# Attending in one bank, a rest behind a root, key features by blocks of 432 and an early bias in an attention kernel

## The chip, the cores and the metric

The kernel runs on one core of one Trainium2 chip. A core has a matrix engine (TensorE: PE for the products, PEld for loading the stationary side), a vector engine (VectorE, DVE), an engine for functions (ScalarE, ACT), a general engine (GpSimd, POOL) and an engine that here only issues transfers (SyncE, SP); 16 DMA engines move data between the device memory and the core's own memory. Products are written to PSUM, which is used in banks of 512 fp32 numbers for each of 128 partitions. The metric is device time in microseconds (us) from the first to the last instruction of one launch; lower is better. All arithmetic here is fp32.

## The reference, cut to what matters

Eight images of 128 channels and 36 x 36 pixels pass through two layers. Layer 0 is an attention between convolutions. Layer 1 turns the image into N = 1296 tokens of C = 128 numbers, attends additively over all pairs of tokens and sends the result through experts that pick their tokens:

```python
# layer 1, attention (x is the normalized token t)
q = einsum('bld,ed->ble', x, Wq) + bq
k = einsum('bld,ed->ble', x, Wk) + bk
t = tanh(q[:, :, None, :] + k[:, None, :, :])
scores = einsum('bijd,d->bij', t, w) + bw[0]
attn = softmax(scores, axis=-1)
return einsum('bij,bjd->bid', attn, x)

# layer 1, experts (E = 64, hidden 512, K = 8 tokens for each expert)
probs = softmax(einsum('bsd,ed->bse', x, gate_w) + gate_b, axis=1)
vals, idx = top_k(probs.transpose(0, 2, 1), K)
gathered = x[flat_idx].reshape(Bn, K, E, Dn)
pooled = einsum('bked,bke->bed', gathered, topv)
h = gelu(einsum('ebd,edh->ebh', [pooled, 1], weight1))
out = einsum('ebh,eho->ebo', [h, 1], weight2)
outputs[b, flat_idx] += out * topv
```

The tanh of a sum over 128 channels for each of 1296 x 1296 pairs is most of the work, and with it the scores.

## The kernel before

**How the tanh becomes products.** With exponentials of the key and of the query, tanh(q + k) is a quotient: for each pair and channel a numerator and a denominator, both sums of few products. The channels' features lie in NF = 8 blocks of 128 rows. For a key tile and a block, TensorE forms the denominators `d` and the numerators `n` of several channels at once, as small products with 32 or 64 rows; ACT takes the logarithm of `d` and the exponential of its negative (`lq`, lines 972 and 975), VectorE multiplies `n` by it (`rp`, line 1003), and POOL adds up the products (line 1012), VectorE for a few slots (lines 997 and 999). The sum gives the scores of one key tile, and ACT its exponential `e` (line 1032).

**Tiling.** The queries of an image are cut into 3 chunks of CH = 432, each of 4 query tiles of T = 108. The keys are cut into KT = 11 tiles, ten of 128 and a rest of REM = 16. A unit is a chunk against a key tile; it has 12 slots (the rest 2). The loop runs over all slots, 2,928 in all. In slot p it calls `numerators(p)` and `denominators(p + LAG)` and `terms`, then gives other work a turn.

**PSUM.** The pool `ps_d` holds the denominators, two tiles of two banks. The pool behind `ps_n` has four banks: a slot takes two for its `n`, and all other work takes its banks from the same pool by `aux(...)`. A bank is handed round when its readers are done.

**Other work, woven in.** Generators do everything that is not a slot, and say at each `yield` what they want next: `step(rest)` and `TAKE` ask for a turn without matmuls, `matmuls(rest)` for one with them; `rest` is the number of slots to wait at least. Four lanes (`first_of_all`, `urgent`, `gates`, `background`) hold the generators. In each slot `take_turns` runs every lane that is due without matmuls, before the numerators, and `matmul_turn` at most one portion of matmuls, behind the denominators, against a budget of 400 columns per slot. `bmm` (line 284) and `turned_to` (line 288) issue a product or a transposition and count its columns. An fp32 product is two matmul instructions in the trace.

**The generators that matter here.**

- `tokens(b)` makes the tokens of the next image, stores them (`tokd`) and leaves normalized tokens `xh` (with a column of ones), their transposition `xT` and the rest's rows `xr`.
- `keys(b, tiles)` (line 667): for each key tile and each half of the feature blocks, four products `pk` of 128 rows by the tile's columns, side by side in one bank, an exponential on ACT (line 687) into `ks`, and a store to `kd` in the device memory, laid out by key tile. For the rest tile POOL multiplies `ks` by two constants (line 692) and only the two products are stored. `made` holds the tiles that are done. `prefetch(u)` (line 926) loads the features `kf` of a unit two units ahead.
- `attend(b, c, es)` runs when all 11 `e` of a chunk are there. It loads the chunk's tokens from `tokd` (four loads on SP), and for each of 4 query tiles `weigh` (line 737) sums the 11 products of `e` and `xh` in two parts of 6 and 5 key tiles, each in a bank `pa` of its own: VectorE copies the first part to `sums` (line 770), adds it to the second (line 772), and adds the sum, divided by its column of ones, to the tokens in `t2` (line 775).
- `attend_early` does nine of the eleven key tiles of the very last chunk while the loop still runs, in two parts as well.
- `gate_logits` (line 793) normalizes the chunk again: POOL takes the inverse root of the variances as a power (`rsqrt`, line 265), TensorE turns `t2` twice, VectorE copies it to `t2T` (line 820, which is stored to `t2d`), normalizes it (line 830) and gets the gate's logits. `gate_tokens` (line 850) makes the softmax, the top 8, the weights `gt` of the chosen tokens (all others zero; stored to `gd`) and the pooled tokens. For the last image the subtraction that gives `gt` is on VectorE.

**The tail.** After the loop, `urgent.run` gives one turn to what is left of `urgent`. Then nine of the 32 expert weights of 1 MB are requested on SP (`load_next`, line 1173), the biases, and what is left of `urgent` is drained. `gates` and `res` are read back for the final sum, and `gate_tokens(7)` runs. In the loop over groups of four experts `inner` forms the first product for a group (a bias by the product with `which`, line 1231, then four products) and its gelu, `turned` transposes, `outer` makes the second product; every weight that is used up makes room for the next. At the end the results are spread over the tokens (`pf`), added to `res` and stored image by image.

Of the kernel before, what the change touches and what calls it, by code (L numbers as in the profile page):

```python
# [23 lines left out]
T = 108  # L24
# [46 lines left out]
def kernel(  # L71
# [43 lines left out]

    kd = [dram.tile([NKT, 128, NF * 128], F32, tag=f"kd{b % 2}", name=f"kd{b}") for b in range(NB)]
    tokd = [dram.tile([N, C], F32, tag=f"tokd{b % 2}", name=f"tokd{b}") for b in range(NB)]
# [12 lines left out]
    with ExitStack() as loop, ExitStack() as score:  # L130
# [455 lines left out]

        prepared, made = {}, set()

# [77 lines left out]

        def keys(b, tiles):

            xT = prepared[b][1]
            yield matmuls(1)  # L670
            for t in tiles:
                o, n = KT[t]
                first = (b, t) == (0, order[0])
                if first:
                    kf_of[0] = kfp.tile([128, NF, 128], F32, tag="kf", name="kf")
                for q0 in (0, NF // 2):
                    some = slice(q0, q0 + NF // 2)
                    pk = aux("pk1").rearrange("p (q t) -> p q t", t=128)
                    for q in range(NF // 2):
                        bmm(pk[:, q, :n], a_k[:, (q0 + q) * 128 : (q0 + q + 1) * 128],  # L680
                           xT[:, o : o + n], start=True, stop=True)
                    yield TAKE
                    if first:
                        ks = kf_of[0][:, some, :]
                    else:
                        ks = kstp.tile([128, NF // 2, 128], F32, tag="ks", name="ks")
                    nc.scalar.activation(ks[:, :, :n], pk[:, :, :n], AF.Exp)
                    kd3 = kd[b][t].rearrange("p (q t) -> p q t", t=128)[:, some, :]
                    if n == REM:

                        for x in range(2):
                            nc.gpsimd.tensor_scalar(
                                ks[:, :, (x + 1) * n : (x + 2) * n], ks[:, :, :n],
                                pairs[:, min(q0, 1), x : x + 1], None, ALU.mult,
                            )
                        nc.sync.dma_start(kd3[:, :, : 2 * n], ks[:, :, n : 3 * n])
                    else:
                        nc.sync.dma_start(kd3, ks)
                    if q0 > 0:
                        made.add((b, t))  # L700
                    yield matmuls()

# [17 lines left out]
        def attend_early(b, c, es):  # L720

            xh, _, xr = prepared[b]
            held = [chunk_tile("sums") for _ in range(TPC // 2)]
            for i in range(TPC):
                at = (i % 2) * (C + 1)
                sums = early[i] = held[i // 2][:T, at : at + C + 1]
                for some in (order[:5], order[6 : NKT - 2] + order[5:6]):
                    pa = aux("pa1")[:T, : C + 1]
                    weigh(pa, i, some, es, xh, xr)
                    yield TAKE  # L730
                    if some[0] == order[0]:
                        nc.vector.tensor_copy(sums, pa)
                    else:
                        nc.vector.tensor_add(sums, pa, sums)
                    yield matmuls()

        def weigh(pa, i, some, es, xh, xr):

            for j in some:
                if j < NKT - 1:  # L740
                    e, v = es[j][:, i * T : (i + 1) * T], xh[:, j, :]
                else:
                    rows = slice(32 * i, 32 * i + REM)
                    e, v = es[j][rows, :T], xr[rows]
                bmm(pa, e, v, start=(j == some[0]), stop=(j == some[-1]))

        def attend(b, c, es):


            xh, _, xr = prepared[b]  # L750
            if c == 0:
                t2 = big_tile("t2").rearrange("p (t c) -> p t c", c=128)
                mv = two.tile([T, NT, 2], F32, tag="t2_mv", name="t2_mv")
                attended[b] = (t2, mv)
            t2, mv = attended[b]
            own = range(c * TPC, (c + 1) * TPC)
            for at in own:
                nc.sync.dma_start(t2[:T, at, :], tokd[b][at * T : (at + 1) * T])
            for i, at in enumerate(own):
                if i in early:  # L760
                    parts, sums = (order[NKT - 2 :],), early[i]
                else:
                    parts = (range(6), range(6, NKT))
                    sums = two.tile([T, C + 1], F32, tag="sums", name="sums")
                for some in parts:
                    pa = aux("pa1")[:T, : C + 1]
                    weigh(pa, i, some, es, xh, xr)
                    yield TAKE
                    if some[0] == 0:
                        nc.vector.tensor_copy(sums, pa)  # L770
                        yield matmuls()
                nc.vector.tensor_add(pa, pa, sums)
                inv = small.tile([T, 1], F32, tag="inv", name="inv")
                nc.vector.reciprocal(inv, pa[:, C : C + 1])
                nc.vector.scalar_tensor_tensor(
                    t2[:T, at, :], pa[:, :C], inv, t2[:T, at, :], ALU.mult, ALU.add
                )
                st = small.tile([T, 6], F32, tag="t2_st", name="t2_st")
                nc.vector.bn_stats(st, t2[:T, at, :])
                nc.vector.bn_aggr(mv[:, at, :], st)  # L780
                yield matmuls()
            if c == NCH - 1:
                prepared.pop(b)
            if b == NB - 1:
                yield from gate_logits(b, [c])
# [7 lines left out]
        def gate_logits(b, chunks):  # L793
# [23 lines left out]
            for c in chunks:  # L817
# [3 lines left out]
                nc.sync.dma_start(t2d[b][:, c * CH : (c + 1) * CH], tt)  # L821
                yield matmuls(1)
                for j0 in range(0, TPC, 2):
# [26 lines left out]
        def gate_tokens(b):  # L850
# [24 lines left out]
            yield step(2)  # L875
            (nc.vector if b == NB - 1 else nc.gpsimd).tensor_sub(gt, pr, gt)
            nc.sync.dma_start(gd[b], gt)
            yield matmuls(3)
            half = NT // 2
            gT = []  # L880
# [45 lines left out]
        def prefetch(u):  # L926
            if u < len(units) and u not in kf_of:
                b, c, j = units[u]
                assert (b, j) in made
                n = 128 if j < NKT - 1 else 32  # L930
                kf = kfp.tile([128, NF, 128], F32, tag="kf", name="kf")
                nc.sync.dma_start(
                    kf[:, :, :n], kd[b][j].rearrange("p (q t) -> p q t", t=128)[:, :, :n]
                )
                kf_of[u] = kf
# [164 lines left out]
        a_q, a_k, cs_s, fb_s, eb_s = (feat[n] for n in ("a_q", "a_k", "cs_s", "fb_s", "eb_s"))  # L1100
        drain(tokens(0), keys(0, order[:1]))
        for i, q in enumerate(IN_TURN):
# [4 lines left out]
        for p in range(LAG):  # L1107
            denominators(p)
        drain(keys(0, order[1:3]))
        prefetch(1)  # L1110
        urgent.append(keys(0, order[3:]))
        pending = deque()
        for p, (u, k) in enumerate(slots):
            b, c, j = units[u]
            rem = j == NKT - 1
            if k == 0:
                prefetch(u + 2)
                if c == 0 and j == 1:
# [4 lines left out]
                    if b + 1 < NB:  # L1123
                        background.extend(
                            (normal(b + 1), conv_keys(b + 1), layer0(b + 1), tokens(b + 1),
                             keys(b + 1, range(NKT)))
                        )
# [56 lines left out]
        urgent.run(len(slots))  # L1184
        for _ in range(9):
            load_next()
        b1_s = biases.tile([E, HID], F32, tag="b1", name="b1_s")
        nc.sync.dma_start(b1_s, weight1[:, 128, :])
        b2_s = biases.tile([128, O], F32, tag="b2", name="b2_s")
        for h in range(2):  # L1190
            nc.sync.dma_start(b2_s[E * h : E * (h + 1)], weight2[:, HID, :])
        drain(*urgent)

# [10 lines left out]
        res.append(big_tile("res")[:, :N])  # L1204
        nc.sync.dma_start(res[4], t2d[4])
        drain(gate_tokens(NB - 1))

# [15 lines left out]
    def inner(g):  # L1223
        ph = aux("phid")

        of_group = ident[:E, g * EG : (g + 1) * EG].rearrange("p (q x) -> p q x", x=1)
        which = hidp.tile([E, EG * 32], F32, tag="which", name="which")
        nc.gpsimd.tensor_copy(
            which.rearrange("p (q x) -> p q x", q=EG), of_group.to_broadcast([E, EG, 32])
        )  # L1230
        mm(ph, which, b1_s, start=True, stop=False)
        for q in range(EG):
# [51 lines left out]
    for h in range(NB // 2):  # L1284
        for c in range(NCH):
# [5 lines left out]
            for i in range(2):  # L1291
                r = res[2 * h + i][:, cols]
                nc.vector.tensor_add(r, pfs[i], r)
        for b in (2 * h, 2 * h + 1):
            nc.sync.dma_start(out[b], res[b])

# [61 lines left out]
```

The softmax here doesn't subtract the row's maximum and nothing guards it: scores larger than these inputs give would overflow.

## Time and profile before

| | us |
|---|---|
| median of three runs (lowest, highest) | 6137.45 (6137.38, 6148.23) |
| the profiled execution | 6140.74 |
| its span, from the first to the last instruction | 6139.0 |
| the loop over the slots in it | 162 to 5986 |
| the first and the last request for a weight of the tail | 5987.38 / about 6094 |
| end of the last addition of results on VectorE | 6132.96 |

The mean granted clock of TensorE was 0.985 of full speed. The costliest groups of instructions (busy us, mean ns of one, then idle time before them and what ended most of it):

```
L1012 POOL TENSOR_TENSOR accp<-accp,rp 128x864 f32<-128x864 f32 x1440 | 2915.8, 2025 | 1041.0 <-DVE rp L1003 948.8
L949 PE MATMUL n<-qf,kf 32*128 32x432 f32 (+1 forms) x11520 | 3325.3, 574 | 46.5 <-ACT e L1032 13.3
L949 PE MATMUL d<-qf,kf 32*128 32x432 f32 (+1 forms) x11520 | 2991.6, 561 | 38.7 <-ACT lq L972 38.2
L972 ACT ACTIVATE lq<-d 128x864 f32<-128x864 f32 x2928 | 2524.2, 878 | 542.6 <-PE d L949 512.1
L1003 DVE TENSOR_TENSOR rp<-n,lq 128x432 f32<-128x432 f32 x3912 | 2173.3, 600 | 743.5 <-PE d L949 542.8
```

A line starts with the line of code, the engine and the operation, then what is written and read, the shape and the number of instructions. Matmuls overlap each other, so their busy time and their means are larger than what one adds to the time. Idle time of an engine that doesn't set the pace costs nothing.

### The profile page before, as it was taken

The numbers are of one execution on the slowest core, as the hardware profiler recorded it, in microseconds if no ns is written. First come the engines' busy times: TensorE is split into PE (matmuls) and PEld (weight loads), VectorE is DVE, ScalarE is ACT, GpSimd is POOL, SyncE is SP. The second block draws the span as 40 slices with busy tenths as digits, with TensorE's granted clock in tenths as the row PEclk, the third lists the DMA queues.
The fourth block names the chain that finished last, engine by engine and source line by source line (L and its number), as shares of the span: only waits on it lengthen the run. The fifth ranks groups of instructions, "written<-read, shape, count | busy, mean of one in ns | idle before, by whom it ended". The sixth has DMA issues, their size and how long they took to land.

```text
span 6139.0 us, 93072 instructions
## 1 busy us (share of the span) xinstructions
PE 5957.9 (97%) x33480; PEld 2862.1 (47%) x33480; DVE 4796.4 (78%) x9521; ACT 5279.9 (86%) x5371; POOL 4597.7 (75%) x2819
## 2 busy tenths in 40 slices
PE   7999999999999999999999999999999999999996
PEld 5454444544544445444455444454444544544443
DVE  4787878877788787877888777887778877788882
ACT  1888898888988888889998889888898888999990
POOL 4777777777787777778778786877777777787870
PEclk9999999999999999999999999999999999999997
DMA  1210011100110002100111001110011100110008
GB/s 44 70 37 22 25 62 38 34 25 28 68 43 20 26 27 71 39 24 23 44 55 39 22 24 59 44 39 22 20 65 40 34 25 28 58 50 29 28 20 297
DMA packets 151519, 270.87 MB, mean 44 GB/s; under 512 B 45648, under 2 KB 76752, under 8 KB 151056
## 3 DMA queue, kind: packets, MB, share of 16 engines
q1 hardware_dynamic: 151056, 264.92, 13.0%
q8 instruction: 264, 4.33, 0.3%
q14 instruction: 199, 1.63, 0.1%
HBM read 200.41 MB, written 64.19 MB: 43 GB/s over the span
## 4 chain that ended last, share of the span: by engine, by line
PE 77%; ACT 7%; DVE 6%; issue 6%; POOL 2%; DMA 1%; SPq 0%; DVEq 0%; POOLq 0%; ACTq 0%
PE n L949 37%; PE d L949 12%; PE pa L284 7%; PE pc L284 5%; ACT lq L972 5%; PE s L284 3%; PE pk L284 3%; PE pq L284 3%; DVE rp L1003 2%; DVE n L997 1%; DVE accd L999 1%; PE d L954 1%; ACT lq L975 1%; DMA w<-in_weight_dram 1%; PE n L954 1%
## 5 line engine op out<-in xcount | busy, mean ns | idle before, releaser
L1012 POOL TENSOR_TENSOR accp<-accp,rp 128x864 f32<-128x864 f32 x1440 | 2915.8, 2025 | 1041.0 <-DVE rp L1003 948.8
L949 PE MATMUL n<-qf,kf 32*128 32x432 f32 (+1 forms) x11520 | 3325.3, 574 | 46.5 <-ACT e L1032 13.3
L949 PE MATMUL d<-qf,kf 32*128 32x432 f32 (+1 forms) x11520 | 2991.6, 561 | 38.7 <-ACT lq L972 38.2
L972 ACT ACTIVATE lq<-d 128x864 f32<-128x864 f32 x2928 | 2524.2, 878 | 542.6 <-PE d L949 512.1
L1003 DVE TENSOR_TENSOR rp<-n,lq 128x432 f32<-128x432 f32 x3912 | 2173.3, 600 | 743.5 <-PE d L949 542.8
L975 ACT ACTIVATE lq<-lq 128x1728 f32<-128x1728 f32 (+1 forms) x1464 | 2398.2, 1638 | 46.3
L949 PEld LDWEIGHTS n<-qf,kf 32*128 32x128 f32 (+1 forms) x11520 | 1206.4, 184 | 1600.3 <-DVE rp L1003 581.5
L949 PEld LDWEIGHTS d<-qf,kf 32*128 32x128 f32 (+1 forms) x11520 | 1090.0, 185 | 422.1 <-issue 224.7
L997 DVE TENSOR_TENSOR n<-n,lq 128x432 f32<-128x432 f32 x1440 | 814.9, 608 | 142.1 <-PE n L949 88.5
L999 DVE TENSOR_TENSOR accd<-n,accd 128x432 f32<-128x432 f32 x1440 | 866.3, 602 | 24.6
L1010 POOL TENSOR_TENSOR accp<-rp 128x864 f32<-128x864 f32 x240 | 485.2, 2022 | 197.7 <-DVE rp L1003 195.6
L711 POOL TENSOR_SCALAR qf<-qf,cs_s 128x432 f32<-128x432 f32 x192 | 260.9, 1365 | 45.0 <-ACT qf L710 44.4
L284 PEld LDWEIGHTS pa<-xh,e 128*108 128x108 f32 x1920 | 222.5, 174 | 131.1 <-DVE rp L1003 56.0
L1021 POOL TENSOR_TENSOR accd<-accp,accd 128x432 f32<-128x432 f32 x240 | 265.2, 1105 | 18.8
L1019 POOL TENSOR_TENSOR accp<-accp 128x432 f32<-128x432 f32 x240 | 264.4, 1102 | 16.7
L284 PE MATMUL pa<-xh,e 128*108 128x129 f32 x1920 | 262.9, 283 | 8.7 <-ACT e L1032 5.2
L284 PE MATMUL s<-q,k 128*116 128x432 f32 x480 | 230.3, 568 | 1.7 <-DVE q L316 1.4
L284 PEld LDWEIGHTS pk<-xT,a_k 128*128 128x128 f32 x1408 | 171.2, 192 | 107.0 <-DVE n L997 33.7
L462 POOL TENSOR_TENSOR tot<-tot,e 116x432 f32<-116x432 f32 x192 | 212.0, 1104 | 6.0 <-ACT e L471 4.6
L471 ACT ACTIVATE e<-s 116x432 f32<-116x432 f32 x240 | 124.9, 520 | 98.3 <-PE s L284 97.9
L284 PE MATMUL pa<-e,vw 116*128 116x432 f32 x480 | 204.6, 549 | 0.0
L284 PE MATMUL pk<-xT,a_k 128*128 128x128 f32 (+1 forms) x1408 | 202.5, 287 | 0.1
(213 smaller groups left out, 3788.4 us busy)
## 6 DMA issues: line engine op xcount, KB each, us to landing
kf<-kd SPq DMA_DIRECT2D x239, 512.0 KB
kd<-ks SPq DMA_DIRECT2D x158, 256.0 KB
w<-in_weight_dram SPq DMA_DIRECT2D x32, 1024.0 KB
wk_t<-wk_t_d SPq DMA_DIRECT2D x7, 768.0 KB
wv_t<-wv_t_d SPq DMA_DIRECT2D x7, 768.0 KB
wq_t<-wq_t_d SPq DMA_DIRECT2D x7, 768.0 KB
x<-in_x_dram SPq DMA_DIRECT2D x8, 648.0 KB
t<-tokd SPq DMA_DIRECT2D x96, 54.0 KB
```

The source lines that it names most:

```text
L284: mm(out, lhsT, rhs, **kw)
L711: nc.gpsimd.tensor_scalar(qf[:, 1, :], qf[:, 0, :], cs_s[:, q : q + 1], None, ALU.mult)
L949: mm(outs[h][:, :CH], kf[rows[h], q, :], qf_of[b, c, q][rows[h], part, :], start=True, stop=True)
L972: nc.scalar.activation(lq[:, o : o + n, :], d[:, :n, :CH], AF.Ln)
L975: nc.scalar.activation(some, some, AF.Exp, scale=-1.0)
L997: mult(ns[h], ns[h], lq[:, o + h, :])
L999: nc.vector.tensor_add(live["d"], ns[h], live["d"])
L1003: mult(rp[:, h, :], n, lq[:, o + h, :])
L1010: nc.gpsimd.tensor_add(live["p"], live["r"], rp)
L1012: nc.gpsimd.tensor_add(live["p"], live["p"], rp)
L1019: nc.gpsimd.tensor_add(s[:, 0, :], s[:, 0, :], s[:, 1, :])
L1021: nc.gpsimd.tensor_add(d, s[:, 0, :], d)
```

## The change

- `keys` no longer goes by key tiles but by ranges of columns, `keys(b, lo, hi)`: for each of the 8 feature blocks one product over the whole range (432 columns for images 1 to 7; 128, 384, 384, 16 and 384 for image 0), one exponential, one store. `kd` is laid out by feature block and column, so that a load of `kf` takes 128 columns of each block. The rest's products go to a tile of their own, `kr`, by two POOL instructions for each block, and to `krd`.
- `weigh` is a generator that yields after each four products and asks for a turn without matmuls behind the last. `attend` sums all 11 key tiles in one bank `pa`; the copy to `sums` goes, and the addition stays only for the tiles that `attend_early` began, which sums its nine key tiles in one bank too.
- In `gate_logits` the first chunk of an image (but the last image) rests 4 slots instead of 1 behind the store of `t2T`, before the transpositions whose results line 830 normalizes with the root.
- In the tail the biases are requested ahead of the nine weights; for the first two groups the bias product is issued ahead of `gate_tokens(7)`; the subtraction for the last image's `gt` is made in two halves; and the last two images' results are stored chunk by chunk.

```diff
+    kd = [dram.tile([128, NF, N], F32, tag=f"kd{b % 2}", name=f"kd{b}") for b in range(NB)]
+    krd = [dram.tile([128, NF, 2 * REM], F32, tag=f"krd{b % 2}", name=f"krd{b}") for b in range(NB)]
...
-        def keys(b, tiles):
+        def keys(b, lo, hi):
...
+            for q in range(NF):
+                pk = aux("pk1")[:, :n]
+                bmm(pk, a_k[:, q * 128 : (q + 1) * 128], xT[:, lo:hi], start=True, stop=True)
+                yield TAKE
+                ks = kf_of[0][:, q, :] if first else kstp.tile(
+                    [128, CH], F32, tag="ks", name="ks")[:, :n]
+                nc.scalar.activation(ks, pk, AF.Exp)
+                nc.sync.dma_start(kd[b][:, q, lo:hi], ks)
+                if hi == N:
+
+                    for x in range(2):
+                        nc.gpsimd.tensor_scalar(
+                            kr[:, q, x, :], ks[:, n - REM :],
+                            pairs[:, q // (NF // 2), x : x + 1], None, ALU.mult,
+                        )
+                yield matmuls()
+            if hi == N:
+                nc.sync.dma_start(krd[b], kr.rearrange("p q x t -> p q (x t)"))
...
-                for some in (order[:5], order[6 : NKT - 2] + order[5:6]):
-                    pa = aux("pa1")[:T, : C + 1]
-                    weigh(pa, i, some, es, xh, xr)
-                    yield TAKE
-                    if some[0] == order[0]:
-                        nc.vector.tensor_copy(sums, pa)
-                    else:
-                        nc.vector.tensor_add(sums, pa, sums)
-                    yield matmuls()
+                pa = aux("pa1")[:T, : C + 1]
+                yield from weigh(pa, i, order[: NKT - 2], es, xh, xr)
+                nc.vector.tensor_copy(sums, pa)
+                yield matmuls()
...
-            for j in some:
+            for x, j in enumerate(some):
...
-                bmm(pa, e, v, start=(j == some[0]), stop=(j == some[-1]))
+                last = x == len(some) - 1
+                bmm(pa, e, v, start=(x == 0), stop=last)
+                if last:
+                    yield TAKE
+                elif x % 4 == 3:
+                    yield matmuls()
...
+                pa = aux("pa1")[:T, : C + 1]
+                yield from weigh(pa, i, order[NKT - 2 :] if i in early else order, es, xh, xr)
                 if i in early:
-                    parts, sums = (order[NKT - 2 :],), early[i]
-                else:
-                    parts = (range(6), range(6, NKT))
-                    sums = two.tile([T, C + 1], F32, tag="sums", name="sums")
-                for some in parts:
-                    pa = aux("pa1")[:T, : C + 1]
-                    weigh(pa, i, some, es, xh, xr)
-                    yield TAKE
-                    if some[0] == 0:
-                        nc.vector.tensor_copy(sums, pa)
-                        yield matmuls()
-                nc.vector.tensor_add(pa, pa, sums)
+                    nc.vector.tensor_add(pa, pa, early[i])
...
-                yield matmuls(1)
+                yield matmuls(1 if c > chunks[0] or b == NB - 1 else 4)
...
+            if b == NB - 1:
+                for cols in (slice(0, half * T), slice(half * T, N)):
+                    nc.vector.tensor_sub(gt[:, cols], pr[:, cols], gt[:, cols])
+            else:
+                nc.gpsimd.tensor_sub(gt, pr, gt)
...
-                    kf[:, :, :n], kd[b][j].rearrange("p (q t) -> p q t", t=128)[:, :, :n]
+                    kf[:, :, :n], kd[b][:, :, o : o + n] if j < NKT - 1 else krd[b]
...
-        drain(tokens(0), keys(0, order[:1]))
+        drain(tokens(0), keys(0, 0, 128))
...
-        drain(keys(0, order[1:3]))
+        drain(keys(0, 128, 512))
         prefetch(1)
-        urgent.append(keys(0, order[3:]))
+        for lo, hi in ((512, 896), (N - REM, N), (896, N - REM)):
+            urgent.append(keys(0, lo, hi))
...
-                             keys(b + 1, range(NKT)))
+                            + tuple(keys(b + 1, o, o + CH) for o in range(0, N, CH))
...
         urgent.run(len(slots))
-        for _ in range(9):
-            load_next()
         b1_s = biases.tile([E, HID], F32, tag="b1", name="b1_s")
...
+        for _ in range(9):
+            load_next()
         drain(*urgent)
...
+        for g in range(2):
+            biased(g)
         drain(gate_tokens(NB - 1))
...
+            if h == NB // 2 - 1:
+                for b in (2 * h, 2 * h + 1):
+                    nc.sync.dma_start(out[b][:, cols], res[b][:, cols])
+        if h < NB // 2 - 1:
+            for b in (2 * h, 2 * h + 1):
+                nc.sync.dma_start(out[b], res[b])
```

`biased(g)` takes a bank, makes `which` on POOL and issues the bias product, as `inner` did before; `inner` calls it only for groups that have no bias yet.

## The prediction

> **What bounds the kernel now.** I read the page's summary first, then the chain, then the waits, and only then single stretches of time.
>
> ```profile
> PE 5957.9 (97%) x33480; PEld 2862.1 (47%) x33480; DVE 4796.4 (78%) x9521; ACT 5279.9 (86%) x5371; POOL 4597.7 (75%) x2819
> ...
> PE 77%; ACT 7%; DVE 6%; issue 6%; POOL 2%; DMA 1%; SPq 0%; DVEq 0%; POOLq 0%; ACTq 0%
> ```
>
> TensorE is in use for 97% of the span and holds 77% of the chain that ended last; the DMAs hold 1%. So an edit counts if it shortens matmuls or lets them start sooner. The loop of slots runs from 162 to 5986 us, the tail of experts after it. Next, what matmuls wait for, from the view of waits (us in total, times, longest):
>
> ```profile
> PEld n L949 <- DVE rp L1003: 581.5, 1032, 1.5
> ...
> ACT lq L972 <- PE d L949: 512.1, 665, 3.3
> ...
> PEld n L949 <- DVE accd L999: 198.5, 472, 1.6
> ```
>
> Numerators (n) wait for a bank that VectorE must empty: 581.5/1032 = 0.56 us each time. VectorE, not on the chain by its sum, paces TensorE through the banks. Last, three stretches of one batch, by windows (length, then PE, PEld, DVE, ACT, POOL busy, clock, DMA share, GB/s):
>
> ```profile
> 1564.00:1614.00 50.00, 50.00 (x324) 28.18 (x317) 35.02 (x64) 48.24 (x55) 32.76 (x18) 1.00 0.27 96
> 1650.00:1688.00 38.00, 37.83 (x254) 22.11 (x256) 31.82 (x71) 32.95 (x32) 27.81 (x18) 1.00 0.18 62
> 1688.00:1735.00 47.00, 44.95 (x240) 21.65 (x238) 44.92 (x95) 41.84 (x41) 37.02 (x22) 1.00 0.10 29
> ```
>
> The first makes key features: ACT is busy 48.24 of 50, it sets the pace. The second attends (the products pa): PE is full, ACT is at 87%, DVE at 84%. The third is the gating: DVE is busy 44.92 of 47, it sets the pace.
>
> **Part 1, attending in one bank.** The groups by form:
>
> ```profile
> L770 DVE COPY sums<-pa 108x129 f32<-108x129 f32 x92 | 26.6, 289 | 15.3 <-PE pa L284 14.1
> L772 DVE TENSOR_TENSOR pa<-pa,sums 108x129 f32<-108x129 f32 x96 | 28.0, 292 | 11.1 <-PE pa L284 10.7
> ...
> L830 DVE TENSOR_SCALAR t<-tp,t_mv,t_rs 108x128 f32<-108x128 f32 x96 | 34.5, 401 | 7.4 <-POOL t_rs L265 6.6 <-POOL which L1228 0.8
> ```
>
> The 92 copies go, and 92 of the 96 adds (four query tiles still join an early sum): 26.6 + 92 x 0.292 = 53.5 us of DVE. The products pa stay. How much of it reaches the path? At least nothing, where ACT covers it; at most 53.5, since each copy stands between a product and the rp multiply that frees a bank. DVE is at 84% and 96% in the two stretches where attending lies, nearer to full than to idle, but PE itself is full in the first; I take half, -27 us.
>
> The price: one bank of the four that n and all other work share is now held over 3 turns of 4+4+3 products instead of being emptied after 5 or 6. In program order, the n pairs that must take the bank of the pair just before rise from 1,654 to 1,923, by 270. Bounds: 0, and 270 x 0.56 = 151 us if each became a full wait of the row above. In this trace such tight pairs idle no longer than the others (167 ns against 188 ns before the weight load, averaged over both kinds), so I take the lower end with 20 ns each, +5.
>
> **Part 2, the rest behind the root.** L830 is the first reader of the power that POOL computes, and waited 6.6 us for it in 7 batches, with the bank of tp held; the view of that tile's instructions says who waited for it (us, times):
>
> ```profile
> PEld n L949: 17.2, 26
> PE n L949: 10.3, 16
> ```
>
> The first chunk now rests 4 slots instead of 1. Gain between 0 (the work returns later) and 6.6 + 10.3 = 17; I take -7, the DVE row, as DVE sets this stretch. The gating ends three slots later, which nothing awaits before the next batch.
>
> **Part 3, key features by blocks of 432.** Per batch, 88 products of 128 or 16 columns (two matmul instructions each) become 24 of 432. The row of that shape is pq:
>
> ```profile
> L284 PE MATMUL pk<-xT,a_k 128*128 128x128 f32 x1280 | 185.4, 289 | 0.1
> L284 PE MATMUL pk<-xT,a_k 128*128 128x16 f32 x128 | 17.0, 265 | 0.0
> L284 PE MATMUL pq<-xT,a_q 128*128 128x432 f32 x384 | 190.0, 577 | 0.0
> ...
> L687 ACT ACTIVATE ks<-pk 128x512 f32<-128x512 f32 x158 | 92.3, 586 | 1.2 <-PE d L949 1.2
> L471 ACT ACTIVATE e<-s 116x432 f32<-116x432 f32 x216 | 112.2, 519 | 97.4 <-PE s L284 97.0
> L692 POOL TENSOR_SCALAR ks<-ks,pairs 128x64 f32<-128x64 f32 x32 | 13.7, 446 | 6.8 <-ACT ks L687 6.8
> ```
>
> PE: from its first start to the next work's start, a portion of eight pk instructions takes 1.09 us in the trace (0.99 for 16 columns), a portion of two for pq 0.925. So 20 x 1.09 + 2 x 0.99 = 23.8 us per batch become 24 x 0.925 = 22.2, -13 over eight batches. ACT: 20 x 0.586 + 2 x about 0.2 = 12.1 us per batch becomes 24 x 0.519 = 12.5, +3 over all. Because ACT is 96% busy in this stretch, PE's 13 us hide behind it: 0, bounds -13 and +3. Also hidden: the stores grow from 176 to 216, on SP, which nothing on the chain waits for; the 16-column rest takes 128 POOL products instead of 32. From 446 ns for 64 columns and at most that for 16, POOL gets up to 128 x 0.446 - 13.7 = +43 us, in an engine idle 25% of the span whose sums are due 7 slots later; if that cover is gone, +43 at most. I take +3.
>
> Loads of kf now come in 1,024 lines of 512 B. From two stretches, the token store in 512 B lines against loads in 4 KB lines:
>
> ```profile
> 1509.00:1511.00 2.00, 2.00 (x15) 0.99 (x14) 1.96 (x7) 1.63 (x3) 0.77 (x2) 1.00 0.44 124
> 1511.00:1513.00 2.00, 1.61 (x9) 0.59 (x6) 1.91 (x8) 2.00 (x3) 1.56 (x1) 1.00 0.76 208
> 1590.00:1593.00 3.00, 3.00 (x20) 1.96 (x22) 2.97 (x6) 2.97 (x3) 2.92 (x2) 1.00 0.62 206
> 1593.00:1596.00 3.00, 3.00 (x25) 1.58 (x20) 1.33 (x4) 2.78 (x4) 2.29 (x3) 1.00 0.44 168
> ```
>
> (0.44 + 0.76) x 2 = 2.4 us for 664 KB, or 1.9 us per 524 KB, against (0.62 + 0.44) x 3 = 3.2 us for 1,122 KB, or 1.5. The 0.4 us lie in a lead of two units, some 40 us: nothing.
>
> **Part 4, the start.** The loop's first n now waits for eight products of 384 columns; by pq's portion 8 x 0.925 x 384/432 = 6.6 us, at least 8 x 0.577 = 4.6, against 3.8 for the sixteen of 128 columns there today (158.1 to 161.9 us): +2.
>
> **Part 5, the tail.** SP's timeline (start, us, form):
>
> ```profile
> 6000.06 2.76 SPq L1178 DMA_DIRECT2D w<-in_weight_dram  x1
> 6002.92 2.83 SPq L1188 DMA_DIRECT2D b_s<-in_weight_dram  x1
> 6005.79 1.24 SPq L1191 DMA_DIRECT2D b_s<-in_weight_dram  x2
> 6007.13 0.53 SPq L821 DMA_DIRECT2D t2d<-t2T  x1
> 6007.70 19.89 SPq L1200 DMA_DIRECT2D gates<-gd  x21
> ```
>
> Early biases take 2 x 2.0 us off PE's end of the gating, the halves half of a 1.5 us subtraction, the chunked output at most 1.5 us: -6. But attending the last chunk early takes 12 turns now instead of 8, so the single urgent turn ahead of the nine 1 MB weights no longer reaches `attend`, and its four token loads are issued behind these weights on SP. In the trace the weights drain until some 6013.5 (9 x 1.05 MB at the 387 GB/s of that stretch); the first gate loads also stand until 6015. The residual, needed at 5993.9 (L775), would come near 6013.5, and the t2d store with all 24 gate and 3 residual loads behind it near 6020 instead of 6007. That is 13 us on SP; since gate loads need 0.64 us each once the weights are gone, 21 x 0.64 + 8 after 6020 ends near 6042 instead of the 6037.2 of the trace: +5, and the early biases and halves are then covered. The bias loads, moved ahead of the weights, delay these by at most 2.83 + 1.24 = 4.1 us, and no expert can start before the gating ends. Bounds -6 and +13; I take +6.
>
> The Trainium skill, "DMA: Bandwidth & Descriptors", section "Queues, rings and completion order", says that each DMA engine consumes descriptors in ring order. The trace agrees in the gate loads, which stand until 6015. It speaks against this change: by the rule the token loads wait for all nine weights, by a reading without it they would pass them, and the tail would be 6 us shorter than before.
>
> **Sum.** -27 + 5 - 7 + 0 + 3 + 2 + 6 = -18, on 6140.7 of the profiled run (span 6139.0): 6122.7. The median of the runs is 3.3 below that run, so 6119.
>
> **Rivals.** (a) No change: ACT's 86% covers the 53.5 us, since DVE work of one slot may end before ACT's logarithm frees the next; then -7 + 5 + 3 + 2 + 6 = +9, about 6146, at best 6130 if the gating's gain is 17 and the tail's loss 0. For: 512.1 us of waits between ACT and d. Against: n waits more for DVE than for anything else. (b) Slower: the bank held. If one of the 270 pairs costs over 18/270 = 0.07 us more than I said, the gain is gone; at half a full wait, 270 x 0.28 = 76 instead of 5, 6119 + 71 = 6190. For: the row of 0.56 us. Against: tight pairs idle no longer today. (c) The diff speaks of gains at the end and makes a loss: token loads, then gates, all late by 13, 6126.
>
> **How the numbers follow.** Forecast 0.50, (a) 0.20, (b) 0.24, (c) 0.06. A measurement tells 0.2% from no change, 12 us: same is 6125 to 6150. The forecast's own range is 6095 to 6135; adding (a) and half of (b), 6085 to 6165. Faster: 0.50 of the forecast and part of (a), less its upper edge: 0.50. Same: most of (a), (c): 0.23. Slower: (b) and an edge: 0.27.
>
> **What would show it.** Right: no L770 group, 53 us less DVE, waits of n for rp near 560, the POOL wait of L830 gone, pk near 100 us with ACT still above 95% there, token loads of the last chunk issued behind the weights and their residual near 6013. Wrong: n's waits for DVE well over 600 us; or DVE 53 us less, and ACT's idle up by as much.

## The result and the profile after

The changed kernel takes 6210.0 us (median; 6209.27 to 6210.77), the kernel before 6137.4 beside it: a ratio of 1.0114, 95% interval 1.0096 to 1.0131. It is 73 us slower, where 18 us less were forecast. Its profiled span is 6209.1 us.

The page's summary of the changed kernel, the answer to the first lines of the prediction:

```profile
PE 6008.8 (97%) x32488; PEld 2759.6 (44%) x32488; DVE 4763.2 (77%) x9334; ACT 5283.3 (85%) x5403; POOL 4620.7 (74%) x2915
...
PE 81%; ACT 7%; issue 5%; DVE 4%; POOL 2%; DMA 1%; SPq 0%; DVEq 0%; POOLq 0%; ACTq 0%
```

VectorE has lost work (33 us of busy time, 187 instructions) and 2% of the chain; TensorE, with 992 instructions fewer, is busy 51 us longer and holds 81% of the chain. The waits of the changed kernel (us in total, times, longest):

```profile
PEld n L944 <- DVE rp L998: 582.1, 1043, 1.7
PEld n L944 <- issue: 299.2, 657, 1.2
...
PEld pa L285 <- issue: 183.6, 489, 0.6
```

The numerators wait for VectorE as long as before (582 against 581), though VectorE has less to do. So the sign that the prediction named for a costly bank, waits well over 600 us, is not there; what the bank costs shows only against a kernel with the same portions (below). Waits "for issue", in which the profile shows nothing that the engine waited for, rose from 247.5 to 299.2 us ahead of n and from 61.2 to 183.6 ahead of pa. The groups by form that answer to the prediction's:

```profile
L285 PE MATMUL pk<-xT,a_k 128*128 128x432 f32 x336 | 166.8, 578 | 0.1
L685 ACT ACTIVATE ks<-pk 128x432 f32<-128x432 f32 x168 | 87.2, 519 | 0.0
L690 POOL TENSOR_SCALAR kr<-ks,pairs 128x16 f32<-128x16 f32 x128 | 39.7, 328 | 14.7 <-ACT ks L685 12.4 <-DVE rp L998 2.3
L820 DVE TENSOR_SCALAR t<-tp,t_mv,t_rs 108x128 f32<-108x128 f32 x96 | 34.5, 403 | 0.8 <-POOL which L1211 0.8
```

The key features cost ACT what was said (519 ns each), POOL 26 us more, and the wait of the normalization for POOL's power is gone. TensorE's 166.8 us for `pk` are what the prediction's row of pq gives (190.0 x 336/384 = 166), not its "near 100". VectorE's busy time fell by 33 us, not by 53.5: its instructions overlap. The rest of the time went elsewhere. It can be placed by the first logarithm of each image in the trace. The columns, in us, are the first image, the mean of images 2 to 7, the eighth image, and the time from the last logarithm to the end, worked out from the traces of this and the later kernels (the names at the right are those of the runs below; each trace is one execution, so that a row can differ from its median by some us):

```
                        image 1   images 2-7   image 8   behind
before                    746.7        736.9     658.7    155.9
changed                   754.2        741.1     678.2    174.4
changed, rest tile last   750.8        737.5     678.8    173.4   e1_rest_last
 and three banks          745.8        732.3     671.6    172.1   e5_three_banks_last
 three banks              749.1        736.7     676.3    171.9   e3_three_banks
 two portions             753.1        743.2     663.4    162.3   e2_two_portions
 one portion              759.8        749.2     671.8    161.5   e4_one_portion
 token loads first        751.7        741.6     678.2    163.5   c1_hoist
before, keys by blocks    753.5        736.7     663.3    156.5   b2_keys
before, one bank          748.7        737.1     663.5    156.0   b1_one_bank
before, tail's edits      747.5        736.8     657.7    161.3   b4_tail
before, rest of 4         749.8        745.5     661.7    157.9   b3_rest
before, rest of 2         748.2        734.8     659.0    158.7   r2_rest2
before, background early  750.7        745.1     659.7    156.9   ph_early
rest of 2, even slots     740.8        732.2     658.6    157.3   q2_even
```

The 70 us of span are 7.5 at the start, 6 x 4.2 in the middle images, 19.5 in the last image, which has no background work, and 18.5 behind the loop.

### The profile page after: what moved, and what is told of

It is laid out like the page before. It is cut to its first block, busy times and chain, and to the rows that moved or that the text cites. A ratio compares the mean times of both kernels' runs of the same rounds, so it can differ in the third digit from the quotient of the medians.

```text
span 6209.1 us, 91198 instructions
## 1 busy us (share of the span) xinstructions
PE 6008.8 (97%) x32488; PEld 2759.6 (44%) x32488; DVE 4763.2 (77%) x9334; ACT 5283.3 (85%) x5403; POOL 4620.7 (74%) x2915
## 4 chain that ended last, share of the span: by engine, by line
PE 81%; ACT 7%; issue 5%; DVE 4%; POOL 2%; DMA 1%; SPq 0%; DVEq 0%; POOLq 0%; ACTq 0%
PE n L944 41%; PE d L944 12%; PE pa L285 8%; PE pc L285 5%; ACT lq L967 5%; PE s L285 3%; PE pk L285 3%; PE pq L285 3%; DVE rp L998 1%; DVE n L992 1%; PE d L949 1%; ACT lq L970 1%; PE n L949 1%; DMA w<-in_weight_dram 1%; PE px L285 1%
## 5 line engine op out<-in xcount | busy, mean ns | idle before, releaser
L285 PE MATMUL pa<-xh,e 128*108 128x129 f32 x1920 | 310.3, 292 | 7.3 <-ACT e L1027 4.1
L285 PE MATMUL pk<-xT,a_k 128*128 128x432 f32 (+3 forms) x416 | 191.9, 551 | 2.4 <-ACT ks L685 2.4
L285 PE MATMUL pq<-xT,a_q 128*128 128x432 f32 x384 | 189.9, 577 | 0.4 <-DVE rp L998 0.4
```

The costliest lines, as they stand in the source:

```text
L285: mm(out, lhsT, rhs, **kw)
```

## The experiments

Times below are medians; in brackets stand the ratio to the kernel before on the same chip (6137 to 6144 us in all groups) and its 95% interval. A batch is the stretch of slots of one image, a portion what one matmul turn issues of other work. The expectations set theories against each other, each under a letter.

### The changed kernel, attending taken apart

The first theory was that TensorE pays a fixed price for each passage from the small products n and d to full-height ones. The trace of the changed kernel showed such prices; weight loads by timeline (start, duration, form, idle time before):

```profile
5839.64 0.26 PEld L285 LDWEIGHTS pa<-xh,e 128*108 128x108 f32 x2 [0.62 <-issue]
5840.04 0.26 PEld L285 LDWEIGHTS pa<-xr,e 16*108 16x108 f32 x2
5840.43 0.49 PEld L285 LDWEIGHTS pa<-xh,e 128*108 128x108 f32 x4
```

The first weight load of a portion stands 0.62 us behind the load ahead of it. From the load of a product of xh to that of the 16-row rest tile (xr), now the sixth of eleven, it is 0.40 us, and 0.39 us from there to the next product of xh; from one product of xh to the next it is 0.20 to 0.22 us in the single records of the trace (a product is two loads). The Trainium skill, "TensorEngine Tiling (Array Packing)", section "Key Properties", has a rule for it: a change of the tiling mode drains TensorE. The trace agrees at the rest tile, 0.40 us against 0.20 to 0.22. The 0.62 us are no such price: at 5842.81 us a load of 64 rows stands 0.53 us behind another load of 64 rows.

**Rest tile last.**

```diff
-yield from weigh(pa, i, order[NKT - 2 :] if i in early else order, es, xh, xr)
+yield from weigh(pa, i, order[NKT - 2 :] if i in early else range(NKT), es, xh, xr)
```

Expected of e1_rest_last:

> The changed kernel, with the 16-row rest tile last in each query tile's sum instead of sixth of eleven. Theory S (switches): TensorE pays for each passage between the small products n, d and full-height products; the trace of the changed kernel shows about 0.09 + 0.09 + 0.09 us around a rest in the middle, so 92 x 0.27 = 25 us come back, 6185. Theory H (the held bank makes n wait): nothing changes, 6210.

Measured 6184.6 us (1.0075, 1.006 to 1.009): 25 us back, as the theory of switches said. In the traces the next product for n starts 7 ns behind an instruction of a rest tile that is last, but some 200 ns behind a product of xh that is last. Before the change the rest was last; its place moved with the new loop over `order`.

**Two portions, one portion.**

```diff
-                elif x % 4 == 3:
+                elif x == 5:
```

Expected of e2_two_portions:

> The changed kernel, still one bank, but portions of 6 + 5 products instead of 4 + 4 + 3. S: a passage to the portion and back costs 0.62 us whatever its size, 4 fewer per chunk, 23 x 4 x 0.62 = 57 us less; early attending takes 8 turns again, so the token loads go ahead of the weights and the tail gives back about 12: 6141. H: the bank is held over two portions instead of three, about a third of the 57 us of the loop comes back: 6180.

Expected of e4_one_portion:

> The changed kernel with all eleven products of a query tile in one portion, one bank. S: 4 portions per chunk instead of 12: 23 x 8 x 0.62 = 114 us less and 12 in the tail, 6085; less gain if a burst of 2.4 us starves ACT. H: no bank is held, the 57 us of the loop and the tail come back: 6141.

Measured 6202.5 (1.0105, 1.0089 to 1.0122) and 6243.3 (1.0175, 1.016 to 1.019). Fewer passages did not bring 57 and 114 us. In the table e2's last image and tail did recover (663.4 and 162.3), its middle images became worse (743.2). These two runs are not clean: in the program's order both start the next image's background in slot 33 of a batch instead of 36, which costs by itself (see "The phase"). So it is c2 below, with two portions and slot 36, that decides on the fixed price per portion.

**Three portions, each in a bank of its own,** first with the rest in the middle, then with the rest last:

```diff
+                    parts = (order[:4], order[4:8], order[8:])
...
+                for x, some in enumerate(parts):
+                    pa = aux("pa1")[:T, : C + 1]
+                    yield from weigh(pa, i, some, es, xh, xr)
+                    if x < len(parts) - 1:
+                        if x == 0:
+                            nc.vector.tensor_copy(sums, pa)
+                        else:
+                            nc.vector.tensor_add(sums, pa, sums)
+                        yield matmuls()
+                nc.vector.tensor_add(pa, pa, sums)
```

Expected of e3_three_banks:

> The changed kernel, portions of 4 + 4 + 3 as in it, but each in a bank of its own that VectorE empties at once (copy, add, add). S: as many passages as in the changed kernel and 55 us of DVE more: 6210 to 6235. H: no bank is held, the loop is as before: 6150.

Expected of e5_three_banks_last:

> The changed kernel with three portions in banks of their own and the rest tile last. The rest in the middle cost 25 us where one bank was held (6210 to 6184.6), and the held bank 34 with the rest in the middle (6210 to 6176.1). If the two costs are independent: 6151. If the rest in the middle only hurts because the bank is held longer: 6176.

Measured 6176.1 (1.0063, 1.0048 to 1.0078) and 6146.0 (1.0013, 1.0004 to 1.0023). With more work for VectorE the kernel is 34 and 39 us faster than with one bank: the held bank costs that much net, and the rest in the middle 25 to 30 whatever the banks. In the traces every portion of the changed kernel and of e3 lies in the same slot, through all images, and so it is with e1 and e5: nothing differs but the banks and VectorE's copies and additions. The two costs are about independent, as e5's first expectation had it. The waits of e1 (one bank), of e5 (three), both with the rest last, and of e3 (three, the rest in the middle; the changed kernel's line is above):

```profile
PEld n L944 <- DVE rp L998: 594.4, 1062, 1.7
```

```profile
PEld n L955 <- DVE rp L1009: 530.8, 953, 1.7
```

```profile
PEld n L955 <- DVE rp L1009: 531.4, 952, 1.7
```

Holding one of four banks makes the numerators wait 109 times more, 64 us, or 0.58 us for each (91 times and 51 us with the rest in the middle). That is the price and the row of the prediction's rival (b).

**Token loads ahead of the weights.**

```diff
+        while len(urgent) > 1:
+            urgent.run(len(slots))
         urgent.run(len(slots))
         b1_s = biases.tile([E, HID], F32, tag="b1", name="b1_s")
```

Expected of c1_hoist:

> The changed kernel, but what is left of the early attending is drained ahead of the weights, so that the four token loads are issued in front of them on SP. If these loads behind 9 MB of weights cost the tail 12 us (164 us from the first bias load to the end against 152): 6198. If not: 6210.

Measured 6199.0 (1.0089, 1.0074 to 1.0104): 11 us back, and by the traces all behind the loop (174.4 to 163.5). The changed kernel's SP, then its VectorE, by timeline:

```profile
6046.86 1.69 SPq L1174 DMA_DIRECT2D w<-in_weight_dram  x3
...
6057.80 4.63 SPq L1174 DMA_DIRECT2D w<-in_weight_dram  x1
6062.77 4.10 SPq L757 DMA_DIRECT2D t<-tokd  x4
```

```profile
6075.39 0.35 DVE L765 SCALAR_TENSOR_TENSOR t<-pa,inv,t 108x128 f32<-108x128 f32 x1 [29.03 <-DMA t<-tokd]
```

VectorE was idle for 29 us ahead of the first residual, until a token load of 54 KB from behind nine weights of 1 MB had landed. This agrees with the ring order that the prediction weighed. But SP itself issued the weights until 6062.4, 15.6 us from the first; how much of the delay is the issuing and how much the order, no run separates.

### The kernel before, one edit at a time

Expected of b1_one_bank:

> The kernel before with one edit: the two parts of 6 and 5 products are summed in one bank, in the same two portions and the same order (rest last); the 92 copies go and 92 of the 96 adds. If VectorE's 53 us were on the path: 6085 to 6115. Theory S (only passages count): 6137, no change. Theory H (a held bank makes n wait): 6150 to 6170.

Expected of b2_keys:

> The kernel before with the key features by blocks of 432 alone, the start included. The windows of the changed kernel show about 9 us lost in the first 61 slots and 3 to 5 us won in each later batch where the features are made: 6137 + 9 - 7 x 3 to 5 = 6111 to 6125. If the engine for functions hides the gain, as the prediction had it: 6139 to 6146.

Expected of b3_rest:

> The kernel before with the rest of 4 slots behind the root alone. As predicted: -7, 6130. If the work only comes later: 6137.

Expected of b4_tail:

> The kernel before with the edits of the tail alone (biases first, two bias products early, gt in halves, results by chunks); attending is the old one, so that its token loads stay ahead of the weights. From the tails of the changed kernels where those loads are ahead (152 to 153 us from the first bias load to the end, against 151.6 before): 6137 to 6139; the prediction's -6 would be 6131.

The edits are those of the change; in b1 the portions stay 6 + 5:

```diff
-                for some in parts:
-                    pa = aux("pa1")[:T, : C + 1]
-                    weigh(pa, i, some, es, xh, xr)
+                pa = aux("pa1")[:T, : C + 1]
+                for x, some in enumerate(parts):
+                    weigh(pa, i, some, es, xh, xr, x == 0, x == len(parts) - 1)
```

**One bank:** 6149.3 (1.0019, 1.0009 to 1.0028). VectorE has 184 instructions less (34 us of its busy time by the page), every portion lies in its old slot, and yet the time rises by 12. The numerators wait longer, against 581.5 us in 1,032 cases before:

```profile
PEld n L948 <- DVE rp L1002: 612.9, 1076, 1.6
```

**Keys by blocks:** 6150.3 (1.0021, 1.0012 to 1.0031), 13 us slower, above both expectations; its trace shows the loss in the first image (+6.8) and the last (+4.6), and nothing won in the middle (736.7 against 736.9).

**The tail's edits:** 6145.4 (1.0009, 1.0000 to 1.0019), no gain but rather a loss, and above both expectations; behind the loop its trace has 161.3 us against 155.9.

**The rest of 4 slots,** one number, is the surprise: 6194.6 (1.0091, 1.0076 to 1.0106), 57 us slower, though its profile shows the wait for the root gone:

```profile
L830 DVE TENSOR_SCALAR t<-tp,t_mv,t_rs 108x128 f32<-108x128 f32 x96 | 34.5, 402 | 0.7 <-POOL t_rs L265 0.6
```

### Why a rest costs 57 us

By the starts of the numerators, counted from the image's first slot, the rest of 4 is 3.7 us ahead of the kernel before at the point of the old wait (slot 29 of the fourth image), 3.9 behind it at slot 98, 2.5 at slot 121 and 6.5 in the last slot; the other middle images go the same way. Two other rests:

```diff
-                yield matmuls(1)
+                yield matmuls(1 if c > chunks[0] or b == NB - 1 else 2)
```

Expected of r2_rest2:

> The kernel before with a rest of 2 slots behind the root instead of 4 (or 1). Theory P (crowding): ACT leaves room for about one portion of other work per pair of slots, a second one in a pair costs about 1 us. The order of the program has 48 doubled pairs per batch here, 53 with the rest of 4, 49 before, and nothing behind the transpositions moves; 1 to 3.5 us of the wait for the root go in 7 batches: 6113 to 6130. Theory L (later gating itself is what costs): 6137 to 6160.

Expected of r5_rest5:

> The kernel before with a rest of 5 slots. P: 51 doubled pairs per batch, between before (49) and the rest of 4 (53): below the 6195 of the rest of 4, 6125 to 6165. L: the gating is later still, 6195 or more.

A rest of 2: 6132.0 (0.9982, 0.9972 to 0.9991), faster. A rest of 5: 6194.5 (1.0085, 1.0069 to 1.0100). The count of doubled pairs (theory P) foresaw only that the first is faster, and missed the second by 30 us or more; theory L missed the first. With the four places mended together:

Expected of c2_mended:

> The changed kernel mended at four places: portions of 6 + 5, rest tile last, a rest of 2 slots, token loads ahead of the weights. P: 50 doubled pairs per batch instead of 56; start 7, one bank 5, keys 0, rest -7 to -24: 6120 to 6145. If the single edits' losses add up as measured one by one (12 + 13 + 8, less the rest's gain): 6150 to 6165.

Measured 6160.6 (1.0030, 1.0020 to 1.0039), 50 us better than the changed kernel and still slower than before: the sum of the single edits' losses foresaw it, theory P did not. Against e1 less the 11 us of the token loads (6174), two portions instead of three and the rest of 2 bring 13 us together, not 57: the theory of a fixed price per portion falls.

**The slot behind which a portion lands.** In the traces ACT sets an undisturbed pair of slots (two logarithms, then one exponential, 0.77 + 2.46 us from slot to slot). This pacing prefers portions behind even slots:

```diff
-                    paced = balance[0] < 0 or k + 1 in DVE_PAIRS
+                    paced = balance[0] < (PACE // 2 if k % 2 else -PACE) or k + 1 in DVE_PAIRS
```

Expected of q2_even:

> The kernel before with the rest of 2, and a pacing that prefers portions behind even slots (behind an odd slot a portion of the three lanes needs half a turn of credit, behind an even one it may overdraw by one). Theory Q (cover): behind an even slot a portion delays denominators that are covered by a logarithm and an exponential, 0.88 + 1.64 us, behind an odd slot by one logarithm alone; over pairs of slots the traces give some 0.9 us for a portion behind an odd slot and 0.2 behind an even one. 33 portions move to even slots, doubled pairs go from 48 to 43 per batch: 6132 - 33 x 0.7 = 6109. If the place of a portion in its pair is nothing: 6132.

Expected of q6_even_rest4:

> The kernel before with the rest of 4 and the same preference for even slots. Q: the 45 portions of conv and attending that move behind even slots give back 30 to 40 us of the 57: 6155 to 6165. Theory K (clock): the rest's cost is that TensorE's clock is halved more often (60 stretches of 8 us below full clock against 40), whatever the slots: 6180 or more.

Expected of q9_mended_even:

> The mended changed kernel (two portions, rest tile last, rest of 2, token loads first) with the same preference for even slots: doubled pairs 44 per batch against 50. Q: 20 to 25 us less than its 6160.6, 6136 to 6141. If the place is nothing: 6160.

Expected of q7_even_alone:

> The kernel before with the preference for even slots alone (the rest stays 1). Theory Q: the move of 30 portions behind even slots is worth its 22 to 25 us without the rest of 2 as well: 6113 to 6120. If it needs the shorter wait for the root: 6130 or more.

Measured: q2 6107.6 (0.9949, 0.9934 to 0.9964), the fastest kernel of the study; q6 6157.7 (1.0033, 1.0020 to 1.0045), both within what theory Q said. But q9 6160.4 (1.0036, 1.0023 to 1.0050) gained nothing, and q7, the preference without the rest of 2, is 6180.2 (1.0070, 1.0055 to 1.0085), slower by 43. Parity alone does not carry it.

**The phase.** The program's order shows what these kernels share. The first product of the next image's background (`pm`, in `normal`) lies in slot 36 of each middle batch in the kernel before, in the changed kernel, in e1, e3, e5, b1, b2, b4, c1, c2, r2, q2 and q9; their middle images take 732.2 to 741.6 us each. It lies in slot 33, 39 or 30 in b3, e2, e4, q6 (33), r5 (39) and q7 (30): 739.5 to 749.2, each with edits of its own. In b3 the background comes three slots earlier, because the lane of the gating rests and lets it pass. The last run starts the background six slots earlier and changes no work:

```diff
-            yield step(4)
+            yield step(4 if b == 0 else 1)
             st = small.tile([C, NCH, 6], F32, tag="gn_st", name="gn_st")
```

Expected of ph_early:

> The kernel before, with one rest of the next image's first generator (normal, ahead of its statistics) 1 slot instead of 4: in the program's order the whole background then runs six slots earlier through the batch, with the same portions; attending and gating stay in their slots. Theory F (phase): all kernels whose background starts at slot 36 of a batch lie within some +/-30 us by their own edits, all that start at 30, 33 or 39 lost 7 to 8 us in each batch (q7 starts at 30 as this one): 6170 to 6190. Theory L (what costs is that gating ends later) and theory Q (only the slots' parity counts): 6130 to 6145.

Measured 6192.2 (1.0088, 1.0071 to 1.0105): 53 us slower with no work changed and the gating in its old slots, 2 us above what theory F said. Attending did not all stay, as had been expected: in the fourth image's trace some of its portions in the second chunk lie one or two slots later, and parts of the background up to 27 slots earlier. So where the woven work lies in the slots can by itself cost about what the rest of 4 cost. Which property of the placing sets the price is open. A part goes with TensorE's clock: of the windows of 8 us from 160 us to the end, 60 of b3's lie below a granted clock of 0.985 against 40 before (the time in these windows times the share that was not granted is 114 against 81 us), but only 45 (88 us) in ph_early.

## Why the prediction was wrong

- **Attending, "I take half, -27 us".** This step failed. The edit alone, one bank with the old portions, gave +12 (b1) where the prediction's two terms for it, -27 and +5, give -22; whether any of the saved work reached the path by itself no run separates, but it did not pay for the bank. It was also less than 53.5 us: VectorE's busy time fell by 34. Shares of busy time (84%, 96%) said that VectorE was full; what TensorE waits for is a bank, and the removed copy was what set it free.
- **The held bank, "the lower end with 20 ns each, +5".** The mechanism was right, the size wrong, and it is the largest single term: 34 to 39 us net with three portions, against a bank for each. The average over pairs that shared a bank already (167 against 188 ns) was no guide; the row of 0.56 us was: 109 more waits at 0.58, where the prediction had counted 270 more pairs in the program's order. Rival (b) had the place and the row; its price, 76 us instead of 5, stands against 64 us of waits.
- **A term that was missing.** The prediction let the products of pa stay. Their order did not: the rest tile moved to the middle, 25 us. Its working compared counts, not order.
- **More portions per chunk.** The prediction put no price on them in the loop. The last image is 19.5 us longer with 12 portions per chunk and 4.7 with 8 (e2), but 13.1 with 4 (e4), so that the number alone does not set it. The trace of the changed kernel shows slots of up to 6 us there, where the gating in `attend` is drained at the next chunk's second exponential; that this drain makes a difference is argued, not tested by itself.
- **The rest behind the root, -7.** The wait went, as said. That the work behind it "returns later" was bounded at 0; it moved the background's phase, and cost 57 alone with the old attending; a rest of 2, which leaves the phase, is 11 us faster than before. In the changed kernel the three portions keep the phase at 36, so that the rest's harm doesn't show there; this is read from the order of its program, not tried with the rest taken out.
- **Keys, 0, with +3 for POOL; loads of 512 B lines, nothing.** Right for the middle images: 736.7 against 736.9. The edit as a whole cost 13 (b2): the start was +2 in the prediction and +6.8 over the first image, whose background starts in slot 30 instead of 41, and the last image's +4.6 has no explanation here.
- **The tail, +6, bounds -6 and +13.** Right in mechanism and place, too small in size: it is 18.5 us longer. Token loads behind the weights cost 11 (c1); the tail's own edits brought no gain of 6 but, by b4's trace, a loss of some 5.

What was taken back in turn adds up: 6210 less 25 (order), 39 (bank) and 11 (token loads) is 6135, near the kernel before. That it meets the kernel before so closely is in part luck. By its row in the table e5 is 0.9 us shorter than the kernel before in the first image and 4.6 in each middle one, and 12.9 longer in the last image and 16.2 behind the loop. Where the gain in the middle images comes from is open: keys alone won nothing there (b2), and the rest of 4 alone lost (b3). A kernel of e5 with the token loads first was not tried; q2 beats the kernel before, by 0.5%.

## What to carry to other kernels

Where work is woven into a loop at fixed slots, an edit of one rest or one portion can move all that comes behind it; measure such an edit alone, and beside a run that shifts the same work without the edit. A buffer that is held longer is to be priced by the wait that its pool shows already, not by how calm the pool is on average. Count the order of products and of loads, not their number: a rest tile in the middle and 54 KB behind 9 MB cost 36 us here.

## What was not expected of the hardware

Once per image ACT switches to tanh and back. The timeline of the kernel before (start, duration, form), then windows of 2 us (length, PE, PEld, DVE, ACT, POOL busy, clock, DMA share, GB/s):

```profile
1479.41 1.28 ACT L509 ACT_TABLE_LOAD   x1
1480.71 1.38 ACT L509 ACTIVATE hpre<-hpre,hb 128x1296 f32<-128x1296 f32 x1
1482.10 1.28 ACT L510 ACT_TABLE_LOAD   x1
```

```profile
1482.00:1484.00 2.00, 0.00 (x0) 0.00 (x0) 0.01 (x1) 1.97 (x3) 0.66 (x1) 0.88 0.00 0
1484.00:1486.00 2.00, 1.66 (x4) 0.50 (x4) 0.01 (x1) 1.97 (x3) 0.00 (x0) 0.50 0.00 0
1486.00:1488.00 2.00, 2.00 (x8) 0.69 (x10) 1.19 (x3) 1.97 (x3) 0.74 (x1) 0.50 0.00 0
1488.00:1490.00 2.00, 2.00 (x10) 0.76 (x12) 0.87 (x2) 1.98 (x3) 1.27 (x1) 0.50 0.00 0
```

Two table loads and one tanh, 3.9 us, leave TensorE idle for 2.97 us, and its clock then falls to half for 6.8 us. In b3 and in the changed kernel the gap at this place is 4.4 and 4.3 us, with 6.8 and only 3.4 us at half clock behind it: the longer gap does not bring the longer half clock. In b3 the clock halves once more, behind no gap above 0.6 us, after a stretch in which TensorE was busy for 73% to 85% of each 2 us:

```profile
1514.00:1516.00 2.00, 1.46 (x9) 0.44 (x8) 1.97 (x5) 1.97 (x4) 1.96 (x1) 1.00 0.00 0
1516.00:1518.00 2.00, 1.69 (x11) 0.74 (x11) 1.93 (x7) 2.00 (x2) 0.05 (x1) 1.00 0.00 0
1518.00:1520.00 2.00, 2.00 (x7) 1.00 (x6) 1.93 (x7) 0.91 (x2) 1.97 (x1) 0.57 0.00 0
1520.00:1522.00 2.00, 2.00 (x6) 0.50 (x4) 1.97 (x5) 1.21 (x2) 1.95 (x1) 0.50 0.00 0
```

The Trainium skill, "TensorE: Matmul & The Clock Gate", section "HAM oscillation — how this bites in real kernels", gives as the rule that there be no idle gap above some 3.4 us. Here 2.97 us sufficed, and partial idling without any such gap; the measurement decides.
